# Attention scores from split float32r operands in 32x128 tiles, value products in 128x32 tiles, and another order of the work

## The chip, the cores and the metric

The kernel runs on one core of one Trainium2 chip, in one launch. The metric is the device time in microseconds (us): the median of several executions. The engines of a core work side by side, each through its own queue in order: TensorE (PE; its weight loads PEld are shown apart), VectorE (DVE), ScalarE (ACT), GpSimd (POOL) and SyncE (SP), which here issues nearly all DMA transfers.

## The reference, cut to what matters

A hybrid block on x of 8 sequences x 256 tokens x 512 features, fp32. Four layers follow each other, each adding to x: attention with one set of weights, a feed-forward layer, attention with another set of weights, the same feed-forward layer. Each begins with a layernorm.

```python
xq, xk = rope(q), rope(k)                  # 32 query heads, 8 key/value heads, 16 wide
scores = einsum('bhsd,bhtd->bhst', xq, repeat(xk, 4)) / 4
scores = where(causal, scores, -inf)
probs = softmax(scores)
out = einsum('bhst,bhtd->bhsd', probs, repeat(xv, 4)) @ w_o
...
result = x @ base_w.T + base_b             # feed-forward
result += 2 * lora(x, weights of the two best of 8 experts)
```

## The kernel before, in words

A **unit** is one layer pair (attention and feed-forward) of one sequence: 16 units, in the order of four sequences' first pairs, their second pairs, then the other four sequences. A unit has two token halves t of 128.

Every piece of work is given to a planner by `add(engine, cost, tag, function, reads, writes, take, give)`. At the end `Plan.run` issues all pieces in the order of a hand-kept table of due times, TIMES, one number per piece in the order of the `add` calls; LOANS says which buffer of a pool each piece is lent. The costs in `add` don't act in the run. So the order on each engine is fixed beforehand, across units: scores of one unit stand between projections of another, feed-forward products of a third.

Attention of a unit, with its lines:

- Layernorm of each half; four TensorE transposes (L590) turn it, an ACT copy (L597) writes xnT. One of the 64 layernorms (table TURNED) is turned by DVE and DMA instead.
- k (L618) and v (L629) as products, copied to kvs (L637). k is rotated (DVE L643, L645, POOL L667, L669) and copied by ACT with half of each 32 rows set to zero: kz1 (L674), and kz2 (L678), where a row of ones is put in. v goes to vp with ones beside it, by POOL copies (L660) and DMAs (L663).
- q in two pairs of column blocks (L689), rotated by DVE (L703, L706) and POOL (L709, L711), which writes q(0); a DMA copies it to q(1) (L718).
- **First scores**, for the row maximum: five operations (L744), fp32, in 32x64 tiles (32 rows of the array by 64 columns, eight side by side), queries as weights. ACT copies them from PSUM (L759), POOL masks them (L775), DVE takes the negated maximum nm (L789). nm is transposed (L798), copied (L801) and sent by DMA (L805) into a spare row of each head's q.
- **Second scores**, keys as weights, queries streaming: five operations (L830) in 32x64 tiles over 64-key blocks, the spare row adding the negated maximum. ACT takes the exponential (L845), POOL masks diagonal blocks (L856).
- **Value products** (L875) in 64x32 tiles over 64-key blocks, with the sums of the exponentials in the columns of ones; a diagonal block leaves out the query group that lies before it. ACT copies out (L890); the sums go by DMA (L895) to a DVE reciprocal (L898), by DMA to DRAM (L902) and back spread over partitions into rec (L906). DVE merges the two halves (L909) and multiplies (L913). The output product wo follows (L921), and x is added (L928).

The feed-forward layer has a transposed layernorm, gate and lora products (L942), the gate on DVE, a transpose (L992), the base product (L1006) with the lora product on top (L1012), and the addition to x (L1022).

Tiles: `tile_position=(row, column)` says which part of the 128x128 array a product uses. PSUM has eight banks; a score operation takes two pairs of them, a pair holding two tiles' rows of results.

Of the kernel before, what the change touches and what calls it, by code (L numbers as in the profile page):

```python
# [8 lines left out]
F32 = mybir.dt.float32  # L9
U32 = mybir.dt.uint32  # L10
AF = mybir.ActivationFunctionType
# [13 lines left out]
NBIG = 5  # L25
SPLIT = 16
FIXED = 1.65

TURNED = "0000000000000000000000000000000000000000100000000000000000000000"
# [4 lines left out]
0 620 0 620 4960 1860 2480 3100 4340 5950 6695 7300 7660 3720 9430 10050 12530 29775 43837 42597  # L34
31635 27295 19777 10670 8810 11910 31015 17917 43217 8190 13670 20397 19157 18537 32255 11290 29155
13700 14280 22390 23490 0 2000 3707 4707 5707 8227 1550 5390 6707 14505 3150 4510 4610 4850 5610
5910 7307 8022 3900 5290 5740 5980 6565 6865 7767 8522 12767 14527 15457 16642 17490 17860 26610
21017 17297 21410 20700 21680 22865 22455 23275 23775 9227 10997 16370 15150 17190 19430 16387 19077
21712 21102 24070 25340 30395 26675 28467 30042 31042 32330 33660 36372 31367 34192 33192 35277
37682 40534 38857 38077 40302 39302 41642 42752 48982 44232 41067 43322 42322 44477 45267 46122  # L40
34727 37452 35952 38792 39582 41147 50347 50752 52147 51527 50227 50602 52767 50907 55137 57612
56682 59607 66017 58497 60652 59722 61837 63927 61397 63552 62622 65982 67962 68892 64877 66102
67032 68407 69527 67202 69822 71527 70907 74567 75877 75257 77727 73327 81392 86207 90717 70067
71977 73552 74637 76497 78297 79627 80867 82717 76437 89381 91117 99562 91939 92549 94327 96637
97222 97702 100537 101872 107547 108242 109457 113002 113522 114002 114092 114602 114802 115002
115092 116322 117577 104602 120102 121237 100172 101392 102142 103367 103952 107022 109202 109917
111847 114272 115487 115902 118687 116252 119042 119552 119752 119952 120042 120982 121357 110632
131692 132827 9410 10630 10830 11660 12245 13785 18157 19832 10020 10730 10900 11140 17020 17320
18617 19332 20847 22607 23537 24722 25377 25747 58227 57802 27915 52677 27330 28040 29222 29632
41822 32692 29437 32957 35592 34982 36412 40372 24467 26237 28262 29465 29270 30540 44457 45077  # L50
43967 45192 46192 47477 48807 50204 47327 49482 48552 52947 58497 59672 60284 52237 53462 54962
57117 60727 63639 61962 78097 79322 80252 81547 83047 84352 73297 75502 74572 76587 77957 78812
64757 65132 65437 66057 90837 91372 92297 91677 69047 70752 71682 72767 74917 94617 95842 96772
97857 99947 115352 117757 116577 109662 111817 110887 103582 105162 106092 108817 110727 102102
104232 105317 105937 107737 108187 109427 111277 113352 115302 116602 120357 122072 123982 125557
127262 126642 129217 129667 130287 132137 134177 135737 140192 143947 121847 122457 123167 126562
127239 127577 129172 129887 150102 139232 140487 140822 141597 142462 141952 142752 142552 142952
145167 146592 147187 133542 148482 151437 144557 145692 149347 151372 152047 152347 158672 162477
160762 164732 166847 172472 173707 175252 174642 176012 175812 176212 176302 179172 179811 170322
180262 181557 8800 17320 17420 18460 19540 20332 28007 28722 15760 17150 17250 22970 23555 25222  # L60
32337 35122 36317 39047 40137 41322 43356 43726 73887 41977 53387 71917 46057 46767 64552 59252
61582 54462 48297 50467 53194 53844 54577 55847 42037 44937 48332 49594 50137 51407 58422 57182
79067 81182 82112 84287 85617 87172 82337 84492 83562 86947 88327 91327 92649 85237 87392 86462
90857 91967 94397 95009 101097 102372 103302 106757 109937 110792 89867 91522 92522 95057 95847
97352 100417 100792 108807 101097 115232 115667 116592 115972 125302 126577 128297 137647 140747
137182 140667 142207 143362 145452 132572 133797 134797 129632 132447 130857 143692 146257 144917
147862 148982 149362 151017 152172 152792 154947 157652 155792 159502 153972 164667 165852 172822
150762 152512 154087 157032 155172 165972 166422 167042 168892 158882 173432 175512 179427 174032
175152 176512 176752 178791 179091 181302 182377 180612 183032 184247 186252 189187 186602 189542
190052 190252 190452 190542 193222 194477 183992 199262 200557 180037 180647 180747 181882 184444  # L70
186077 187932 188687 203907 189362 190737 191072 191847 191422 193722 194432 194232 194632 194722
196242 196777 219252 224482 225929 18830 19440 27080 28750 29335 31972 35697 36952 22362 26980 28912
31810 36242 38382 46867 47582 74317 77167 76237 78352 81022 82177 106487 80247 79007 88057 89437
93077 94262 93852 100172 99672 53207 56107 58902 58292 70647 80277 59467 62367 64552 65202 67137
79007 101717 102337 97517 98742 100942 102037 103887 105282 121102 122327 123257 124342 125452
126627 127369 153832 155107 156107 157262 158892 163002 160827 169352 170577 172707 173862 174902
176582 163762 165917 164987 167042 167832 170262 174422 176087 177012 176392 182732 186797 187722
187102 179292 181447 180517 183637 184757 192252 194657 193477 195742 197832 195272 197957 196957
198292 199517 200517 201702 203977 202977 205177 206297 200302 201957 203042 203662 205462 206532
205912 208382 207132 212032 214622 219509 205622 207532 211127 212902 212282 214932 215382 216002  # L80
217852 215212 224716 226332 231336 220119 224616 226539 227422 228286 228857 230112 230827 236052
231662 234347 234682 236052 235332 236859 237369 243667 245012 245102 254592 254967 232782 257162
258427 233694 235162 235262 235502 236117 240507 248562 249277 242902 249992 251367 251767 252287
253237 252727 255412 254632 259647 259737 261052 261557 251112 262382 263677 122557 129047 129147
129387 134047 135797 138152 139987 133437 135537 135637 135877 137002 137302 138772 139487 154852
159292 156772 160477 162632 169447 193582 170132 177632 199922 170432 171142 172297 175177 175587
192047 144662 146712 152177 148737 152997 163462 160222 161992 164017 165362 168622 171852 178252
188342 181762 184427 182987 185877 187207 191512 208852 210127 212127 213212 217722 218897 220729
225362 227517 226587 228732 229842 236247 232016 222892 225547 224117 226632 227942 229026 213652
214877 215807 216892 220252 222407 237972 238347 239892 238652 237692 238497 239272 240512 242762  # L90
244987 243987 246072 253862 245662 247817 246887 249682 251772 249022 252487 253487 254712 255937
256867 258172 260327 259397 261412 262687 255682 257797 258882 259502 261487 262557 261937 264407
260682 269972 271052 274967 259142 263882 265537 267242 266622 269042 270112 269492 271962 269322
275577 282262 286177 276982 277592 277692 281262 282197 282497 288662 289537 287592 291052 292267
292602 294157 293562 294512 302197 300427 302517 302707 305022 305397 301542 306572 307867 286787
287397 287497 288862 290157 291037 292012 292727 295422 296942 298317 300627 301147 303497 302987
306647 306136 306847 306937 307612 308837 298062 324852 325987 310852 326767 153222 155227 155327
158372 169317 171577 173962 174677 182167 182777 182877 183117 183702 185357 187472 188187 209872
212722 211792 213907 214562 216512 249412 235502 233022 232706 218832 219542 221437 228447 233847
221847 190482 193502 195527 196177 202637 214562 196522 202722 205872 206522 209757 221042 222377  # L100
234262 230692 231917 232847 234002 237322 238882 239862 242227 241227 247192 248302 251154 249477
316012 317237 318237 319392 320502 321677 322289 343932 346087 345157 347172 347962 350312 346822
348047 348977 350062 350902 353332 323692 324877 325182 329787 367232 367667 367972 369212 349812
# [991 lines left out]
```

## Time and profile before

| | us |
|---|---|
| median of 3 runs | 775.36 |
| runs | 774.77 to 775.43 |
| span of the profiled execution | 775.9 |
| PE busy, L744 / L830 / L875 | 89.6 / 89.9 / 78.5 |
| PE busy, L689 / L921 / L1006 | 124.5 / 117.0 / 116.4 |

The page gives no time for the profiled execution beyond its span, which lies 0.5 us above the median of the runs. A busy time counts an engine's instructions from start to end, overlaps once; instructions of TensorE overlap, so a line's share is only roughly its cost. "x16" counts instructions: an fp32 product of TensorE is two. The granted TensorE clock has a mean of 0.996. In a timeline a row is a run of like instructions: start, length, engine, line, operation, tile names, tile shape, count, and in brackets the idle time ahead of it and what ended it.

### The profile page before, as it was taken

How to read it: one execution, taken by the hardware profiler on the slowest of the kernel's cores; microseconds unless marked ns; L12 is line 12 of the kernel's file. 1: busy time of each engine (PE TensorE's matmuls, PEld its weight loads, DVE VectorE, ACT ScalarE, POOL GpSimd, SP SyncE). 2: the span in 40 equal slices, each digit the busy share in tenths (PEclk: the TensorE clock that was granted, in tenths of full speed). 3: DMA queues.
4: the chain of work that ended last, by engine and by line, in shares of the span. 5: the costliest groups of instructions: out<-in, count | busy, mean ns of one | idle time of the engine just before them, and what ended most of it. 6: DMA issues, size and time to landing. Idle time of an engine off the chain costs nothing.

```text
span 775.9 us, 18093 instructions
## 1 busy us (share of the span) xinstructions
PE 761.0 (98%) x7192; PEld 410.1 (53%) x7192; DVE 489.4 (63%) x1036; ACT 493.1 (64%) x826; POOL 507.0 (65%) x495
## 2 busy tenths in 40 slices
PE   7999999999999999999999999999999989999998
PEld 6865554564555455546555465355555435444344
DVE  5394866468668547556748468556974883465654
ACT  3679675657767664685665657747478676657631
POOL 3899983677666776466847468664758975646530
PEclk8999999999999999999999999999999999999999
DMA  9631100011010010121022210011001100111111
GB/s 293 174 101 34 35 31 18 17 46 34 17 44 22 3 48 15 37 56 49 30 73 69 68 53 18 5 45 34 16 22 46 56 3 19 39 41 45 31 45 54
DMA packets 49395, 36.59 MB, mean 47 GB/s; under 512 B 30624, under 2 KB 34208, under 8 KB 49312
## 3 DMA queue, kind: packets, MB, share of 16 engines
q1 hardware_dynamic: 48768, 35.42, 15.6%
q8 instruction: 56, 0.92, 0.5%
q14 instruction: 27, 0.22, 0.1%
q10 hardware_dynamic: 544, 0.03, 0.0%
HBM read 19.97 MB, written 4.98 MB: 32 GB/s over the span
## 4 chain that ended last, share of the span: by engine, by line
PE 86%; POOL 5%; issue 3%; ACT 2%; DMA 2%; DVE 1%; SPq 0%; POOLq 0%; ACTq 0%; DVEq 0%
PE banks L689 14%; PE banks L921 13%; PE banks L1006 13%; PE banks L830 9%; PE banks L744 9%; PE banks L875 9%; PE banks L942 4%; PE banks L618 4%; PE banks L590 4%; PE banks L629 3%; PE banks L1012 3%; POOL big L775 2%; POOL big L856 2%; ACT big L845 1%; DMA big<-in_wqkv_a 1%
## 5 line engine op out<-in xcount | busy, mean ns | idle before, releaser
L775 POOL TENSOR_SCALAR_AFFINE_SELECT big<-big 64x1024 f32<-64x1024 f32 (+1 forms) x160 | 170.2, 1063 | 90.8 <-ACT big L759 85.2
L789 DVE TENSOR_REDUCE nm<-big 128x8 f32<-128x512 f32 (+3 forms) x112 | 185.1, 1669 | 47.2 <-POOL big L775 47.2
L759 ACT COPY big<-banks 128x512 f32<-128x512 f32 (+1 forms) x235 | 160.3, 749 | 54.2 <-PE banks L744 50.3
L845 ACT ACTIVATE big<-banks 128x512 f32<-128x512 f32 (+1 forms) x215 | 161.3, 811 | 48.5 <-PE banks L830 44.5
L856 POOL TENSOR_SCALAR_AFFINE_SELECT big<-big 64x1024 f32<-64x1024 f32 (+1 forms) x96 | 142.7, 1488 | 62.3 <-ACT big L845 57.2
L689 PE MATMUL banks<-xnT,wqkv 128*128 128x256 f32 x512 | 124.5, 390 | 0.3 <-ACT big L759 0.3
L921 PE MATMUL banks<-wo,e 128*128 128x512 f32 x256 | 117.0, 600 | 1.0 <-DVE ro L703 0.7
L1006 PE MATMUL banks<-base_sb,yT 128*128 128x512 f32 x256 | 116.4, 598 | 0.0
L689 PEld LDWEIGHTS banks<-xnT,wqkv 128*128 128x128 f32 x512 | 95.0, 193 | 31.7 <-issue 14.7
L830 PE MATMUL banks<-q,kz 32*64 32x512 f32 (+1 forms) x1536 | 89.9, 537 | 2.6 <-ACT lwT L996 1.0
L744 PE MATMUL banks<-kz,q 32*64 32x384 f32 (+3 forms) x2048 | 89.6, 443 | 1.3 <-ACT big L759 1.3
L560 POOL TENSOR_TENSOR st<-st,neg_half 128x1 f32<-128x1 f32 x64 | 35.4, 554 | 75.3 <-DVE st L558 62.4
L875 PE MATMUL banks<-big,vp 64*32 64x512 f32 (+1 forms) x1536 | 78.5, 522 | 0.3 <-ACT big L845 0.3
L563 ACT ACTIVATE xn<-x,st 128x512 f32<-128x512 f32 x64 | 51.9, 817 | 40.0 <-DVE st L561 37.2
L921 PEld LDWEIGHTS banks<-wo,e 128*128 128x128 f32 x256 | 46.4, 190 | 55.9 <-issue 47.7
L1006 PEld LDWEIGHTS banks<-base_sb,yT 128*128 128x128 f32 x256 | 46.3, 190 | 54.0 <-issue 50.1
L744 PEld LDWEIGHTS banks<-kz,q 32*64 32x64 f32 x2048 | 36.6, 130 | 41.0 <-issue 17.0
L875 PEld LDWEIGHTS banks<-big,vp 64*32 64x32 f32 x1536 | 26.2, 106 | 53.9 <-issue 38.6
L554 DVE BATCH_NORM_STATS2 st<-x 128x6 f32<-128x512 f32 x64 | 43.8, 688 | 12.7 <-DMA x<-in_x 11.8
L709 POOL TENSOR_TENSOR ro<-ro,rtab 128x512 f32<-128x512 f32 x32 | 41.2, 1289 | 15.3 <-DVE ro L703 8.4
L890 ACT COPY e<-banks 128x1024 f32<-128x1024 f32 (+1 forms) x39 | 33.1, 864 | 23.1 <-PE banks L875 13.7
L830 PEld LDWEIGHTS banks<-q,kz 32*64 32x64 f32 x1536 | 25.4, 130 | 37.8 <-issue 17.8
(74 smaller groups left out, 876.0 us busy)
## 6 DMA issues: line engine op xcount, KB each, us to landing
q<-q SPq DMA_DIRECT2D x32, 256.0 KB
rec<-recd SPq DMA_DIRECT2D x32, 256.0 KB
x<-in_x SPq DMA_DIRECT2D x16, 256.0 KB
out<-x SPq DMA_DIRECT2D x16, 256.0 KB
big<-in_wqkv_a SPq DMA_DIRECT2D x2, 512.0 KB
big<-in_wq_b SPq DMA_DIRECT2D x2, 512.0 KB
base_sb<-in_base_t SPq DMA_DIRECT2D x4, 256.0 KB
wo<-in_wo_b SPq DMA_DIRECT2D x4, 256.0 KB
```

The source lines that it names most:

```text
L563: add("ACT", 0.82, (u, z + "ln"), lambda: nc.scalar.activation(at("xn", k), xt(b, t), AF.Identity, bias=st(10, 11), scale=st(9, 10)), [xk, ...
L689: nc.tensor.matmul(at("bank", k)[:, (j % 2) * S : (j % 2 + 1) * S], W[:, c, j * P : (j + 1) * P], xnT()[:, c, :], start=(c == 0), stop=(c ...
L744: nc.tensor.matmul(ps[64 * c : 64 * c + 64, base // 256 * 256 : base // 256 * 256 + 2 * dist] .rearrange("p (s k) -> p s k", s=2)[:, :, ba ...
L759: add("ACT", 1.03, (u, f"s1{gr}"), lambda h=h, kb=kb: [nc.scalar.copy(at("big", kb)[:, 2 * h + lo : 2 * h + hi, :], ps) for lo, hi, ps in ...
L775: nc.gpsimd.affine_select(out=v, in_=v, compare_op=ALU.is_ge, fill=MASKED, base=0, pattern=[[0, 2048 // w], [0, blocks * w // 2048], [-1, ...
L789: nc.vector.tensor_reduce(nmv(t)[:, :, m0 : m0 + k, :, g], v, AX.X, ALU.max, negate=True)
L830: nc.tensor.matmul(ps[64 * s : 64 * s + 64, 256 * col : 256 * (col + ng)], kz2()[lo : lo + 32, s, k * P + 64 * h : k * P + 64 * h + 64], q ...
L845: add("ACT", 1.03, (u, f"s2{gr}"), lambda z=z, kb=kb: [nc.scalar.activation(pv_(kb)[:, 2 * z + lo : 2 * z + hi], ps.rearrange("p z (g n) - ...
L856: nc.gpsimd.affine_select(out=v, in_=v, compare_op=ALU.is_ge, fill=0.0, base=0, pattern=[[0, 16 * nm], [1, 64]], channel_multiplier=-1,)
L875: nc.tensor.matmul(ps[s][32 * i : 32 * i + 32, 256 * g : 256 * (g + ng)].rearrange("p (g n) -> p g n", n=256), vp()[64 * s : 64 * s + 64, ...
L921: nc.tensor.matmul(at("bank", ("wo", km)), e()[:, 1, j * P : (j + 1) * P], WO[:, j, :], start=(j == 0), stop=(j == 3),)
L1006: nc.tensor.matmul(ps, at("yT", k)[:, c, :], base_sb[:, c, :], start=(c == 0), stop=False)
```

## The change: what it does

Operands. `half(z)` reads or writes a tile as float32r. A copy into such a view rounds to the part that float32r keeps (high); the value minus it, rounded again, is low.

- k: two shuffles spread each head's 16 rows over 32 (each twice), for s = 0 and 1; ACT writes the high part kh, POOL the low part kl. kz1 and kz2 go.
- q: the rotated q is written in an order with the token blocks outside; ACT writes its high part, DVE its low part, one DMA puts both into DRAM (qd), two fetch them so that each head half s has high and low in alternate rows, 32 rows a head. The copy q(0) to q(1) goes.
- First scores: `qv(s)` times kh, then kl, summed in PSUM; 32x128 tiles, four side by side.
- nm is split in high and low (two DVE operations), transposed together, and sent by one DMA into rows of a tile nmr.
- Second scores: kh, kl, and a third pass of constant selector rows `sel` with nmr, 32x128 tiles, over 128-key blocks, split by s: six operations. The mask is one POOL instruction of 128 partitions per diagonal operation.
- Value products: 128x32 tiles over 128-key blocks, one operation per (t, k, s): six, with nothing left out. vp is written by two POOL copies; its DMAs go.
- The broadcast of the sums goes into the second half of e after the merging copy, and rec goes; the product is made in place. Pools: kvs 2 to 1, nm 4 to 2.
- TURNED goes: every layernorm is turned by TensorE. TIMES and LOANS are new.

```diff
         for s in range(2):
+            add("DVE", 0.45, (u, "krope"), lambda s=s: nc.vector.stream_shuffle(
+                kw()[:, s, :], krc(), [16 * s + d // 2 for d in range(32)]),
+                [(u, "krc")], [(u, "kw", s)], give=[("kr", u)])
+        add("ACT", 0.6, (u, "khl"), lambda: nc.scalar.copy(half(khl(0)), kw()),
...
+        add("POOL", 1.30, (u, "khl"), lambda: nc.gpsimd.tensor_tensor(
+            half(khl(1)), kw(), khl(0), ALU.subtract),
...
+            add("ACT", 0.6, (u, "qhl"), lambda ro=ro, rc=rc: nc.scalar.copy(half(ro()), rc()),
+                [(k, "rc")], [(k, "ro")])
+            add("DVE", 0.69, (u, "qhl"), lambda ro=ro, rc=rc: nc.vector.tensor_tensor(
+                half(rc()), rc(), ro(), ALU.subtract), [(k, "ro")], [(k, "rc")], kind="port")
+            add("SP", FIXED + 1.0, (u, "qhl"), lambda k=k: nc.sync.dma_start(
+                at("qd", k), at("ro", k).rearrange("p h j n -> p (h j n)")),
...
+                    q(s)[:, 2 * jp : 2 * jp + 2].rearrange("p j n -> p (j n)"),
+                    at("qd", k).rearrange("(i s d) (h n) -> s i (d h) n", i=4, s=2, h=2)[s]),
...
+                    for s in range(2):
+                        for h in range(2):
+                            for i in range(4):
+                                lo = 32 * i
+                                ps = at("pair", (kb, i // 2))[i % 2]
+                                nc.tensor.matmul(
+                                    ps[:, base + s * dist : base + s * dist + nk],
+                                    qv(s)[lo : lo + 32, m, 2 * t + g, :],
+                                    half(khl(h))[lo : lo + 32, s, 0:nk],
+                                    start=(h == 0), stop=(h == 1), tile_position=(lo, 0),
+                                )
...
+                for z in range(3):
                     for i in range(4):
                         lo = 32 * i
                         ps = at("pair", (kb, i // 2))[i % 2]
+                        if z < 2:
+                            w = khl(z)[lo : lo + 32, s, k * P : (k + 1) * P]
+                            v = qv(s)[lo : lo + 32, :, 2 * t : 2 * t + 2, :]
+                        else:
+                            w = sel[lo : lo + 32, s, :]
+                            v = half(at("nmr", (u, t)))[lo : lo + 32].rearrange(
+                                "p (g m n) -> p m g n", g=2, m=2)
+                        nc.tensor.matmul(
+                            ps.rearrange("p (g m n) -> p m g n", g=2, m=2), half(w), v,
+                            start=(z == 0), stop=(z == 2), tile_position=(lo, 0),
+                        )
...
+                        for i in range(4):
+                            nc.tensor.matmul(
+                                ps[32 * i : 32 * i + 32].rearrange(
+                                    "p (j g k) -> p g j k", j=4, g=2),
+                                vp()[:, s, k, i, :],
+                                pv_(kb)[:, i].rearrange("p g (j k) -> p g j k", j=4),
+                                start=(k == 0), stop=(k == t), tile_position=(0, 32 * i),
+                            )
```

## The prediction

> **What bounds the kernel now.** I read four views in turn: busy time by engine, the chain that ended last, TensorE alone in order of time, and all engines around one normalisation chain. The first two on the page:
>
> ```profile
> PE 761.0 (98%) x7192; PEld 410.1 (53%) x7192; DVE 489.4 (63%) x1036; ACT 493.1 (64%) x826; POOL 507.0 (65%) x495
> ...
> PE 86%; POOL 5%; issue 3%; ACT 2%; DMA 2%; DVE 1%; SPq 0%; POOLq 0%; ACTq 0%; DVEq 0%
> ```
>
> TensorE is idle for 775.9 - 761.0 = 14.9 us, and the chain lies on it. A third of its work is scores and value products. A "busy" PE includes overlaps, so I price operations from start to start, TensorE alone, in order of time (start us, length us, line, shape, instructions):
>
> ```profile
> 302.50 1.11 PE L744 MATMUL banks<-kz,q 32*64 32x512 f32 x16
> 303.54 1.19 PE L942 MATMUL banks<-gl_sb,yT 128*128 128x136 f32 x8
> ...
> 316.64 3.24 PE L875 MATMUL banks<-big,vp 64*32 64x512 f32 x64
> 319.81 1.11 PE L830 MATMUL banks<-q,kz 32*64 32x512 f32 x16
> 320.86 1.99 PE L618 MATMUL banks<-xnT,wqkv 128*128 128x256 f32 x8
> 322.78 1.12 PE L744 MATMUL banks<-kz,q 32*64 32x384 f32 x32
> 323.83 0.29 PE L798 MATMUL banks<-ident,nm 128*32 128x128 f32 x1
> 323.95 1.06 PE L629 MATMUL banks<-wqkv,xnT 128*128 128x128 f32 x8
> 324.85 3.60 PE L1006 MATMUL banks<-base_sb,yT 128*128 128x512 f32 x8
> 328.28 0.27 PE L992 MATMUL banks<-ident,gl 128*128 128x128 f32 x1
> 328.39 1.06 PE L629 MATMUL banks<-wqkv,xnT 128*128 128x128 f32 x8
> 329.38 1.11 PE L830 MATMUL banks<-q,kz 32*64 32x512 f32 x16
> ```
>
> Four prices come out. (1) An fp32 product is two instructions. Eight of 512 columns take 328.28 - 324.85 = 3.43 us: 0.429 us each, 0.84 ns a column and instruction, 0.857 us a product. (2) Eight instructions with 128 columns and 128 new weight columns take 324.85 - 323.95 = 0.90 us, 0.1125 each. (3) A score operation (16 instructions, eight tiles side by side, so two rounds of 0.429) takes 303.54 - 302.50 = 1.04: 0.857 + 0.18. The value products of one query half (seven full rounds' worth, 3.00) take 319.81 - 316.64 = 3.17: also + 0.17, though four times longer. So tiles run truly side by side and about 0.18 is paid per **run** of tiled work, not per round. (4) The untiled work ahead of a tiled run ends later: L629 takes 0.99 before a score (329.38 - 328.39) against 0.90. Other lines pay up to 0.20 (L618: 1.92 against 8 x 0.215 = 1.72). I use 0.15.
>
> **The change on TensorE, per unit (16 units).** Before: five score operations for the maximum, five for the exponentials, five full-size equivalents of value products (1.5 + 3.5): 15 x 0.857 = 12.86 us.
>
> After, value products: six of four fp32 products, 128x32 tiles, four side by side: 6 x 0.857 = 5.14. It is +0.86 because a 128-key block can't skip the empty half of a diagonal block.
>
> Exponential scores: six operations of three rounds, 512 columns each, float32r. No row shows a float32r pass. The nearest row is one fp32 instruction, 0.429 a round. A quarter of an fp32 product is 0.857/4 = 0.214: an fp32 product multiplies two parts of each operand in two instructions, and the change hands over operands already reduced to one part each, which leaves one of four partial products. I take the quarter for that count; the row's price, half a product, stays as the upper end, and nothing in the trace goes below the quarter. 18 x 0.214 = 3.86, against 4.29.
>
> Maximum scores: groups 0 to 2 have eight rounds of 64 to 192 columns, each with 128 new weight columns. No row of 128 new weight columns is shorter than price (2), so I take 0.1125 a round: 3 x 8 x 0.1125 = 2.70. Groups 3 and 4 have four rounds of 256 columns: 2 x 4 x 0.107 = 0.86. Sum 3.56 against 4.29. From below, at a quarter price throughout, groups 0 to 2 cost 3 x 1024 columns x 0.42 ns = 1.28.
>
> Together 12.56 against 12.86: -0.30, times 16 = **-4.8 us**. Fewer passes are almost eaten by one more score operation, a third pass for the maximum (the sel rows), and one more value product.
>
> **Runs and switches.** Sorting TensorE's operations by the two tables of due times gives 154 runs of scores and 35 of value products before, 157 and 63 after; changes from untiled to tiled work go from 144 to 169. So 3 x 0.18 + 28 x 0.17 + 25 x 0.15 = **+9.1 us**. The sixth value operation and the split by key half s cause it: their weights and masks arrive at different times, and the order lets other work between. A float32r run may pay less or more than 0.18 (its first weights are 128 columns: a load takes 190 ns on L1006, 131 on L744): nothing to twice, +/-28 us over 157 runs.
>
> One layernorm goes back from the DMA to TensorE: **+0.5** (four transposes).
>
> Rule against row: the Trainium skill, "TensorE: Matmul & The Clock Gate", section "Measured speedup vs the span model", has four row tiles of 512 columns only 3.07 times faster, not four. Price (3) has no such loss per round. By that rule the float32r rounds, some 7.4 us a unit, would be 30% longer: about +35 us, an estimate from that page. Its section "The mechanism" lets a weight load overlap only products of another row group. The rounds of L875 in one run show no exposed load; by the rule each of 18 + 32 rounds a unit would show one, with the page's 107 ns for 128 columns about +85 us, again an estimate.
>
> **The other engines.** DVE: 32 shuffles at 0.44 (L643), 32 subtractions at 0.69 (as L706), 64 tiny ones at about 0.16: +46. ACT: four kz passes (rows L674 and L678, 34.8 in all) leave, 48 copies of 128x512 at 0.59 and 16 x 2 exponentials at 1.03 come: +27. POOL: k's subtraction 16 x 1.28 = +20.5; masks 64 x 2.12 = 136 against 142.7. All three stay below 545 us, 70%: none becomes the bound, and TensorE covers their work wherever it has another unit's products next. Without that cover the delay counts.
>
> What lengthens is the path. q used to be ready for scores after the POOL addition (L711). Now a copy (0.59), a subtraction (0.69) and two transfers through DRAM follow. All engines, near the end, price a hop:
>
> ```profile
> 739.31 1.15 SPq L902 DMA_DIRECT2D recd<-sums  x2
> ...
> 741.76 0.61 SPq L906 DMA_DIRECT2D rec<-recd  x1
> ...
> 745.56 0.69 DVE L913 TENSOR_TENSOR e<-e,rec 128x512 f32<-128x512 f32 x1 [1.85 <-DMA rec<-recd]
> ```
>
> The second small write is issued near 739.9 and its reader at 741.76: 1.9. The 256 KB broadcast takes 745.56 - 741.76 = 3.8. So q gains 1.3 + 2 x (1.9 to 3.8) = 5.1 to 8.9 us, say 7; bytes grow by 32 x (1024 - 256) KB, on engines with a 16% share. k gains two shuffles, a copy and a subtraction less two kz passes: about 2. The maxima gain two tiny DVE operations. The output's broadcast (L906) now waits for the masked copy (L909), and what stands behind it on SP waits too; that copy ran at 742.80 here, 1 us after the issue, so about 1 us per half, under other products except in the last units. Transfers of v and the copy q<-q leave; SP's issues stay at eight a unit on this part.
>
> At the start no other unit covers: the first scores stand at 32.46, after q at 29.21. With 7 more they can't start before 36.2: **+4** (0 if products of the next units fill it, 9 if the second unit is late as well). Later, at 600 to 700 us, where the first wave of units runs out, TensorE is idle for 4.1 us; a path longer by about 10 and single instead of double kvs and half as many nm buffers give **+4** more (0 to 25).
>
> **Sum** against the execution's own span: 775.9 - 4.8 + 9.1 + 0.5 + 4 + 4 = 788.7; the median of the runs lies 0.5 below that span, so **788**.
>
> **Rivals.**
> (A) As summed, 780 to 800: 0.52.
> (B) Faster. Weight loads of four row tiles hide behind the round before, so that rounds under 256 columns cost their columns alone: 2.70 becomes 1.28, times 16 = -23, giving 788 - 23 = 765. For it: in L744 eight loads of 64 columns hide in rounds as short as 128 columns (322.78 to 323.83 holds four rounds and still takes 1.05). Against: price (2). It decides from the point where a round of the first three groups costs about 0.08 instead of 0.1125 (384 rounds x 0.033 = 12.7). 0.18.
> (C) The change doesn't get the quarter: a float32r instruction costs as much as an fp32 one, 0.429 a round. 18 x 0.215 + 8 x 0.107 = 4.7 more a unit, +76: 864. For it: the only one-instruction products here, L590's transposes, cost 0.11 per 128 columns. 0.10.
> (D) The longer path or the runs cost several times what I gave: 800 to 825. For it: POOL waits 142 us for ACT behind scores already. 0.13.
> (E) No measurable difference, parts of A and B cancelling: 0.07.
>
> Leaving out C and the lower half of B and the far end of D, the range is 764 to 820. About 0.2% (1.6 us) is what a measurement here can tell from no change. Faster 0.18 (B), same 0.07 (E), slower 0.75 (A, C, D).
>
> **What would show it.** A: exponential scores about 0.64 + 0.18 from start to start, the maximum's first group near 1.08, its last near 0.61; PE busy still 95% or more. B: the first group near 0.65. C: 1.3 + 0.18. D: PE idle over 35 us with q or nmr named. I am wrong if TensorE's runs cost under 0.1, or if idle time falls.

## The result and the profile after

| | median, us | runs, us | ratio to before [95% interval] |
|---|---|---|---|
| before | 775.39 | 774.77 to 775.55 | |
| after | 916.19 | 912.58 to 919.17 | 1.1826 [1.1786, 1.1865] |

The change makes the kernel 18% slower. The profiled execution took 913.86 us, with a span of 912.1. The direction was forecast; the size, 788 with a range to 820, was not.

The page of after: busy time by engine, the granted TensorE clock and the DMA engines' share in 40 slices, and the chain that ended last:

```profile
PE 815.8 (89%) x6044; PEld 474.6 (52%) x6044; DVE 546.6 (60%) x1196; ACT 515.6 (57%) x740; POOL 523.7 (57%) x481
...
PEclk9878999989988999999999999899999998979999
DMA  9432120201102012101221213020120120200001
...
PE 56%; DMA 20%; DVE 12%; ACT 5%; issue 3%; POOL 2%; SPq 2%; DVEq 0%; ACTq 0%; POOLq 0%
```

TensorE falls from 98% to 89% of the span, its clock dips all through the run, and a fifth of the chain lies on transfers, where it was 2%. No other engine is near its limit.

TensorE can be accounted for in full: span = its busy time at full clock + what half clock added (half of the busy time in stretches with a granted clock of 0.50) + its idle time.

| us | span | busy at full clock | added by half clock | idle |
|---|---|---|---|---|
| before | 775.9 | 758.0 | 3.0 | 14.9 |
| after | 912.1 | 776.5 | 39.3 | 96.4 |
| difference | 136.2 | **18.5** | **36.3** | **81.5** |

TensorE's own work, the subject of most of the prediction, is the smallest part. The waits of after that matter, and then the first of them in before (engine, line, waited for, total us, times, longest):

```profile
DVE e L916 <- DMA e<-recd: 73.1, 22, 10.7
...
PE banks L922 <- DVE e L916: 34.7, 13, 7.2
...
PE banks L751 <- DMA q<-qd: 17.8, 4, 7.6
```

```profile
DVE e L913 <- DMA rec<-recd: 25.4, 13, 7.0
```

The largest is not q, whose path got longer, but the broadcast of the softmax sums (e<-recd): DVE waits for it, and the output product (L922) waits for DVE; in before the waits of that product (L921) add up to 1.1 us, none of them for this. One such stall in the chain of waits of after (start, length, what):

```profile
166.56 3.59 DMA qd<-ro
170.16 0.54 SPq L719
...
171.89 10.21 DMA recd<-sums
182.15 3.64 DMA e<-recd
185.81 0.70 DVE e L916
186.65 5.53 PE banks L922 x8
```

The write recd<-sums carries 8 KB, yet lands 10.2 us after it was issued. Just ahead of it SP had issued four fetches q<-qd of 256 KB. Stretches of after around it (busy time and count of PE, PEld, DVE, ACT, POOL; then clock, DMA share, GB/s):

```profile
168.00:170.00 2.00, 2.00 (x24) 1.59 (x21) 1.60 (x1) 0.66 (x2) 2.00 (x3) 1.00 0.79 315
172.00:173.00 1.00, 1.00 (x13) 0.60 (x14) 0.00 (x0) 0.21 (x2) 0.00 (x0) 1.00 0.27 104
180.00:181.00 1.00, 0.00 (x0) 0.00 (x0) 0.00 (x0) 1.00 (x2) 0.00 (x0) 1.00 0.26 100
184.00:185.00 1.00, 0.00 (x0) 0.00 (x0) 0.00 (x0) 0.00 (x0) 0.41 (x1) 0.50 0.49 182
```

While q is written to qd, the DMA engines' share is 0.79. While it is fetched, the share is about 0.26, and the rate 100 GB/s: 256 KB take 2.6 us, four fetches some 10. The fetch reads qd as `"(i s d) (h n) -> s i (d h) n"`: its outermost dimension is four blocks of 32 rows. The Trainium skill, "DMA: Bandwidth & Descriptors", in its rules for kernel authors, says that an outermost dimension of fewer than 16 confines a transfer to at most that many DMA engines; four of 16 is the share seen. From 179.5 on TensorE has nothing to do, and when it goes on at 186.65 it runs at half clock.

TensorE's prices themselves came out close. Timeline of after (start, length, line, shape, count):

```profile
312.69 0.50 PE L843 MATMUL banks<-q,kh 32*128 32x512 f32 x4
313.03 0.40 PE L843 MATMUL banks<-q,kl 32*128 32x512 f32 x4
313.26 0.40 PE L843 MATMUL banks<-nmr,sel 32*128 32x512 f32 x4
313.58 0.66 PE L592 MATMUL banks<-ident,xn 128*128 128x128 f32 x4
314.17 1.06 PE L882 MATMUL banks<-big,vp 128*32 128x512 f32 x8
315.17 0.30 PE L811 MATMUL banks<-ident,nm 128*64 128x128 f32 x1
315.40 1.06 PE L882 MATMUL banks<-big,vp 128*32 128x512 f32 x8
316.40 0.33 PE L751 MATMUL banks<-kh,q 32*128 32x128 f32 x4
...
317.44 0.33 PE L994 MATMUL banks<-ident,gl 128*128 128x128 f32 x1
```

A float32r round of 512 columns takes 0.23 (313.26 - 313.03), a quarter of an fp32 product and a little; an operation of the second scores 0.89 (313.58 - 312.69), a value operation 1.00, the first maximum group 1.04 (317.44 - 316.40) in eight rounds.

### The profile page after: what moved, and what is told of

Read it like the earlier page. It is cut to its first block, busy times and chain, and to the rows that moved or that the text cites. A ratio compares the mean times of both kernels' runs of the same rounds, so it can differ in the third digit from the quotient of the medians.

```text
span 912.1 us, 15854 instructions
## 1 busy us (share of the span) xinstructions
PE 815.8 (89%) x6044; PEld 474.6 (52%) x6044; DVE 546.6 (60%) x1196; ACT 515.6 (57%) x740; POOL 523.7 (57%) x481
## 4 chain that ended last, share of the span: by engine, by line
PE 56%; DMA 20%; DVE 12%; ACT 5%; issue 3%; POOL 2%; SPq 2%; DVEq 0%; ACTq 0%; POOLq 0%
PE banks L922 10%; PE banks L679 9%; PE banks L882 8%; PE banks L1008 7%; DMA e<-recd 6%; PE banks L843 5%; PE banks L751 5%; DMA recd<-sums 4%; DMA q<-qd 4%; DMA qd<-ro 3%; PE banks L592 3%; PE banks L619 2%; PE banks L1014 2%; DVE nm L795 2%; ACT big L765 2%
## 5 line engine op out<-in xcount | busy, mean ns | idle before, releaser
L856 ACT ACTIVATE big<-banks 128x1024 f32<-128x1024 f32 (+1 forms) x207 | 190.7, 963 | 89.1 <-PE banks L843 84.1
L781 POOL TENSOR_SCALAR_AFFINE_SELECT big<-big 64x1024 f32<-64x1024 f32 (+1 forms) x160 | 169.6, 1061 | 116.1 <-ACT big L765 109.2
L765 ACT COPY big<-banks 128x1024 f32<-128x1024 f32 (+1 forms) x176 | 157.1, 943 | 88.9 <-PE banks L751 87.7
L865 POOL TENSOR_SCALAR_AFFINE_SELECT big<-big 128x2048 f32<-128x2048 f32 x64 | 137.7, 2153 | 80.3 <-ACT big L856 73.1
L922 PE MATMUL banks<-wo,e 128*128 128x512 f32 x256 | 128.3, 648 | 35.0 <-DVE e L916 34.7
L679 PEld LDWEIGHTS banks<-xnT,wqkv 128*128 128x128 f32 x512 | 96.3, 195 | 23.5 <-issue 6.8
L882 PE MATMUL banks<-big,vp 128*32 128x512 f32 x768 | 101.1, 630 | 3.2 <-POOL big L865 2.4
L922 PEld LDWEIGHTS banks<-wo,e 128*128 128x128 f32 x256 | 50.4, 206 | 97.9 <-issue 63.8
L581 POOL TENSOR_TENSOR st<-st,neg_half 128x1 f32<-128x1 f32 x64 | 36.2, 570 | 112.8 <-DVE st L579 98.3
L751 PE MATMUL banks<-kh,q 32*128 32x192 f32 (+3 forms) x1024 | 77.4, 308 | 20.8 <-DMA q<-qd 17.8
L751 PEld LDWEIGHTS banks<-kh,q 32*128 32x128 f32 x1024 | 57.9, 201 | 56.5 <-issue 22.2
L751 PE MATMUL banks<-kl,q 32*128 32x192 f32 (+3 forms) x1024 | 68.7, 291 | 0.0
L843 PE MATMUL banks<-q,kh 32*128 32x512 f32 x384 | 55.8, 500 | 4.5 <-ACT big L856 3.5
L751 PEld LDWEIGHTS banks<-kl,q 32*128 32x128 f32 x1024 | 57.3, 203 | 0.0
L843 PEld LDWEIGHTS banks<-q,kh 32*128 32x128 f32 x384 | 22.1, 185 | 55.8 <-issue 29.3
```

The lines of the kernel that those rows point to most:

```text
L679: nc.tensor.matmul(at("bank", k)[:, (j % 2) * S : (j % 2 + 1) * S], W[:, c, j * P : (j + 1) * P], xnT()[:, c, :], start=(c == 0), stop=(c ...
L751: nc.tensor.matmul(ps[:, base + s * dist : base + s * dist + nk], qv(s)[lo : lo + 32, m, 2 * t + g, :], half(khl(h))[lo : lo + 32, s, 0:nk ...
L765: add("ACT", 1.03, (u, f"s1{gr}"), lambda h=h, kb=kb: [nc.scalar.copy(at("big", kb)[:, 2 * h + lo : 2 * h + hi, :], ps) for lo, hi, ps in ...
L781: nc.gpsimd.affine_select(out=v, in_=v, compare_op=ALU.is_ge, fill=MASKED, base=0, pattern=[[0, 2048 // w], [0, blocks * w // 2048], [-1, ...
L843: nc.tensor.matmul(ps.rearrange("p (g m n) -> p m g n", g=2, m=2), half(w), v, start=(z == 0), stop=(z == 2), tile_position=(lo, 0),)
L856: add("ACT", 1.03, (u, f"s2{gr}"), lambda z=z, kb=kb: [nc.scalar.activation(pv_(kb)[:, 2 * z + lo : 2 * z + hi], ps.rearrange("p z (g n) - ...
```

## The experiments

The theory at the start: fetches on a quarter of the DMA engines delay the sums' round trip behind them. The rival: what costs is the longer path itself (more hops and operations), however fast the fetch. Ratios are to the kernel before, timed on the same chip (774.0 to 775.1 us there).

**1. Each fetch as four transfers of 32 rows** (256 issues for 64).

```diff
-    nc.sync.dma_start(q(s)[:, 2*jp : 2*jp+2]..., at("qd", k).rearrange(...)[s])
+    [nc.sync.dma_start(q(s)[32*i : 32*i+32, 2*jp : 2*jp+2]..., at("qd", k).rearrange(...)[s, i])
+     for i in range(4)]
```

> The changed kernel, but each fetch of q from DRAM (four blocks of 32 rows in one transfer, which moved 100 GB/s at a 0.25 share of the DMA engines, 2.6 us each) is four transfers of one block of 32 rows each. Theory 'narrow fetch': the fetches run on a quarter of the DMA engines and hold up what is queued behind them (one 4 KB write of the sums took 10.2 us behind four of them). Then the fetches spread, the idle time of TensorE falls from 96 us to under 40, and the time is 780 to 815 us. Rival 'long path': the added steps from q and k to the scores and the smaller pools make TensorE wait whatever the fetches' speed; then the time stays over 885 us.

870.44 us, ratio 1.1226 [1.1170, 1.1282]: neither theory's number. (The write of the sums carries 8 KB, not the 4 of the expectation.) The chain of this kernel shows why (the first and the last of sixteen issues in a row, then the small write):

```profile
165.83 0.32 SPq L719
...
172.71 0.42 SPq L719
...
173.17 1.77 DMA recd<-sums
```

The small write now lands in 1.8 us instead of 10.2, as the theory has it; but 16 issues of 0.42 us, one after the other, hold SP for 7.3 us (165.83 to 173.12) ahead of it.

**2 and 3. The same bytes, narrow and wide, in the kernel before.** 64 copies of 256 KB from x to unused DRAM, at the place where q is ready; the two kernels differ in the order of the rows alone.

```diff
+    for s in range(2):   # 2: four blocks of 32 rows
+        nc.sync.dma_start(spare[jp].rearrange("(i z r) n -> z i r n", i=4, z=2)[s],
+                          x[b].rearrange("(i z r) n -> z i r n", i=4, z=2)[s])
...
+        nc.sync.dma_start(spare[jp][P*s : P*s+P, :], x[b, P*s : P*s+P, :])   # 3: one block of 128
```

> The kernel before with two more 256 KB copies per q pair (64 in all) from x to an unused DRAM scratch, as four blocks of 32 rows in one transfer; nothing reads the copies and no step of the path changes. 'Narrow fetch' expects that they hold the queue for about 64 x 2.6 = 168 us and delay the sums, the maxima and the copies of q behind them: 800 to 900 us, with waits for the broadcast of the sums. 'Long path' expects 775 to 781, since no path got longer.

> The same as the run with narrow copies, with the same bytes in the same places of the order, but each copy as 128 rows in one block. Both theories expect 775 to 785 us; if it is as slow as the narrow copies, the bytes or the number of transfers matter and not how they spread over the DMA engines.

Narrow: 831.88 us, 1.0734 [1.0696, 1.0771]. Wide: 779.27 us, 1.0063 [1.0045, 1.0080]. Nobody reads these copies, so the 53 us between them come from their shape alone. The waits of the narrow kernel and then of the wide one for the same broadcast, and SP's own for the small write ahead of it:

```profile
DVE e L919 <- DMA rec<-recd: 48.5, 15, 7.9
SPq L912 <- DMA recd<-sums: 48.9, 29, 8.3
```

```profile
DVE e L919 <- DMA rec<-recd: 26.9, 12, 7.3
SPq L912 <- DMA recd<-sums: 28.3, 28, 1.9
```

**4. A wide fetch in the changed kernel.** The columns of q's weights are put in another order, so that the rows that one fetch needs lie together.

```diff
-    at("qd", k).rearrange("(i s d) (h n) -> s i (d h) n", i=4, s=2, h=2)[s]
+    at("qd", k).rearrange("(s r) (h n) -> s (r h) n", s=2, h=2)[s]
```

> The changed kernel with the columns of the q weights ordered by key half s first (16 small copies at the start instead of 8), so that q's rows lie in DRAM as each fetch needs them: one fetch of 128 rows in one block, no further issue, the same bytes. With 32-row fetches SP spent 16 x 0.46 us in a row on issuing, and a write of the sums waited behind that too. Theory 'held queue' (fetches, first by few DMA engines, then by their number, hold the sums and maxima behind them on SP): both hold-ups go, 785 to 815 us, TensorE idle below 40 us. Rival 'long path': the rest of the 96 us over the kernel before belongs to the added steps and smaller pools: over 845 us.

848.42 us, 1.0953 [1.0932, 1.0973]. Its waits for the sums are half of those of after:

```profile
DVE e L917 <- DMA e<-recd: 36.7, 19, 4.5
PE banks L923 <- DVE e L917: 6.2, 6, 1.8
```

The shape of the fetch is worth 68 of the 141 us. That is half: on the number the rival's side was met, and the theory holds for the other half only.

**5. Small issues in the kernel before.** 192 transfers of 2 KB, as many as experiment 1 had over the change (`for s in range(6): nc.sync.dma_start(spare[s], x[b, 0:16, 0:32])` behind the same addition).

> The kernel before with six more transfers of 2 KB (DRAM to an unused DRAM scratch) per q pair, 192 in all: the issues that 32-row fetches add to the changed kernel, nearly without bytes and on no path. 'Held queue' expects 192 x 0.46 = 88 us more issuing on SP, in knots of 2.8 us, to show as 785 to 820 us with waits for the sums; 'long path' expects under 780.

801.32 us, 1.0344 [1.0313, 1.0375]. Issues alone cost 27 us. With 1 and 4 it roughly fits: splitting cures the shape like the wide fetch, and pays 870 - 848 = 22 for its 192 issues.

**6 to 9. The wide fetch without transfers.** Each leaves work out of kernel 4: the write and fetch of q in all units but the first on each buffer (6); the sums' round trip with the reciprocal (7); the maxima's transfer (8); all three (9).

```diff
-    ..., lambda ...: nc.sync.dma_start(
+    ..., lambda ...: fetched() and nc.sync.dma_start(      # 6; None in 7 and 8
```

> The kernel with wide fetches (848 us) without the transfers of q to DRAM and back, but for the first unit in each of the three attention buffers; later units score with the q that lies there. All engine work stays. Theory 'q detour': what is left over the prediction's 788 us is the detour's two hops and its hold on SP (SP waited 76 us for the q subtraction and 41 us for the write): 785 to 805. Rival 'sums behind each other on DVE' (the product with the sums waits for its broadcast and holds the gates behind it): within 8 us of 848.

> The kernel with wide fetches without the round trip of the softmax sums (five transfers and the reciprocal); DVE's merge and product stay, with what lies in e. Theory 'sums on DVE' expects 790 to 815, since no product waits 37 us in all for a broadcast; 'q detour' expects 835 or more.

> The kernel with wide fetches without the transfer of the maxima into nmr, which stays zero; the maxima are still worked out, turned and copied. 'Q detour' and 'sums on DVE' both expect 838 to 848; if it falls below 825, the maxima's path, which starts after the first scores, is what the longer q path pushes out.

> All three left out at once: q's detour, the sums' round trip and the maxima's transfer. If transfers and the queue are the whole rest, TensorE's own work is left: 775.9 - 14.9 + 4.8 + about 10 for longer runs = 776, plus start and end: 778 to 795. If it stays over 815, the rest lies in the engines' own order and waits and not in transfers.

| kernel | median, us | ratio [95% interval] | against kernel 4 |
|---|---|---|---|
| 6 | 843.61 | 1.0911 [1.0875, 1.0946] | -5 |
| 7 | 837.40 | 1.0814 [1.0792, 1.0835] | -11 |
| 8 | 847.74 | 1.0941 [1.0909, 1.0972] | -1 |
| 9 | 837.16 | 1.0815 [1.0791, 1.0840] | -11 |

Kernel 4's own runs spread from 847.1 to 853.2, so the rows of 6 and 8 show little or nothing. Once the fetch is wide, leaving out these transfers gains 11 us, and 63 us over the kernel before remain without them.

**10 and 11. Without the splitting as well.** From kernel 9, 10 also leaves out what DVE does for the low parts (q's subtraction, the split of the maxima); 11 also DVE's shuffles and the ACT and POOL instructions for high and low of q and k, in all units but the first on each buffer.

> The kernel without the three round trips (837 us), less what the change adds on DVE for the low parts: the 32 subtractions of q and the 64 small operations on the maxima. The scores then use stale or zero operands. In its profile TensorE waited about 7 us for the maxima's split and 10 us for the gates on DVE. Theory 'busy DVE': those waits and the half clock after them go, 805 to 822 us. Rival 'order of the work': the new due times leave such gaps whatever DVE does, 830 or more.

> As the run before, and also without the copies to high parts on ACT, the shuffles of k on DVE and the subtraction on POOL, but for the first unit in each attention buffer. 'Busy DVE' expects no more than 10 us under the run before; a theory 'added steps on the path' expects 785 to 800, near TensorE's own work (about 775 at full clock); 'order of the work' expects 820 or more.

10: 827.22 us, 1.0684 [1.0645, 1.0723]. 11: 827.10 us, 1.0690 [1.0645, 1.0734]. DVE's part is worth 10 us, the rest nothing. What TensorE still waits for in kernel 9 and then in kernel 11:

```profile
PE banks L998 <- DVE gl L993: 8.9, 6, 2.5
PE banks L815 <- DVE nm L813: 7.5, 5, 2.5
```

```profile
PE banks L998 <- DVE gl L993: 8.9, 6, 2.5
PE banks L755 <- ACT big L769: 4.5, 10, 0.7
PE banks L847 <- ACT big L860: 2.7, 5, 0.7
```

The split of the maxima (nm) goes, as it must; the gate (gl) and short waits for ACT's copies and exponentials stay, work that the kernel before has too.

**12. A busier DVE in the kernel before:** two reductions of 128x512 more after each rotation of q, 64 in all and 44 us, that nobody reads (`nc.vector.tensor_reduce(spare, wqkv_sb[0][:, 0, 0:D], AX.X, ALU.add)`).

> The kernel before with 64 more DVE reductions of 128x512 behind the two q operations, 64 x 0.68 = 44 us of DVE work that nothing reads: about what the change adds there. 'Busy DVE' expects 785 to 800; 'order of the work' expects 774 to 780, because the old order has the slack.

786.50 us, 1.0141 [1.0112, 1.0170]: 12 us, though DVE is at 68% only. So work on an engine far from its limit is not free here. That it delays what stands behind it in DVE's order is the likely way; no run singles it out.

**13 and 15. Whose queue?** In the changed kernel, with its narrow fetches, ScalarE issues the small transfers (13: L906 and L913) or the fetches (15: L719) in place of SP: `nc.sync` becomes `nc.scalar`.

> The changed kernel with one edit: the write of the reciprocals to DRAM (recd<-sums) and the broadcast back (e<-recd), 96 small issues in all, are given by ScalarE instead of SyncE; the narrow q fetches stay on SyncE. Theory 'order in SyncE's queue': the small transfers no longer stand behind the fetches, the sums write falls from up to 10.2 us to about 2, the waits of DVE for e<-recd fall from 73 us to under 40, and the time falls from 916 to between 840 and 885 (no further than the wide fetch's 848, and with about 96 x 0.5 = 48 us more issuing on ScalarE, of which some shows). Rival 'the DMA engines themselves are occupied by the narrow fetches, whichever queue a transfer comes from': the write stays near 10 us and the time stays above 900.

> The changed kernel with one edit: the 64 narrow fetches q<-qd are given by ScalarE instead of SyncE; their shape stays as it is, four blocks of 32 rows. Theory 'order in SyncE's queue': SyncE is free for the sums, and the time falls from 916 to between 840 and 890, though ScalarE then waits for the qd write ahead of each fetch and DVE or TensorE waits for ScalarE instead. Rival 'occupied DMA engines': above 900.

13: 904.96 us, 1.1663 [1.1639, 1.1688]. 15: 915.29 us, 1.1831 [1.1798, 1.1864]. The theory that the place in SP's queue decides isn't borne out by the times: parting the small transfers from the fetches gains 11 us in one kernel and nothing in the other. The chain of kernel 13, then its stretches:

```profile
172.70 3.72 DMA recd<-sums
...
179.16 7.05 DMA e<-recd
...
187.46 5.36 PE banks L922 x8
```

```profile
178.00:180.00 2.00, 2.00 (x17) 1.03 (x10) 0.57 (x2) 0.16 (x1) 1.84 (x2) 1.00 0.26 102
180.00:182.00 2.00, 1.89 (x17) 1.04 (x15) 0.00 (x0) 1.82 (x3) 0.71 (x1) 1.00 0.44 159
182.00:184.00 2.00, 0.00 (x0) 0.00 (x0) 0.00 (x0) 1.88 (x2) 0.05 (x1) 1.00 0.28 97
184.00:186.00 2.00, 0.00 (x0) 0.00 (x0) 0.00 (x0) 0.00 (x0) 2.00 (x1) 0.51 0.23 76
```

The small write is quicker (3.7 for 10.2), so the queue does count for it; but the broadcast, now free of SP, takes 7.05 instead of 3.64. It ends at 186.2, where it ended at 185.8 in after. The broadcast is narrow itself: its view, `to_broadcast([8, 16, D])`, has eight blocks outermost, and where it ran alone in after its share was 0.49 (184 to 185). Here the share rises to 0.44 after its issue and falls back to 0.28, that of the fetches, until it ends. That fits a transfer part of which goes through at once while the rest waits on the engines that the fetches occupy; the trace doesn't show single engines. The Trainium skill, "DMA: Bandwidth & Descriptors", states that issuing engines share the same 16 DMA engines (section "Issuing engines are not separate DMA queues"); these two runs agree, with 11 us and nothing gained.

The two runs do not price the queue alone, since each moves waits elsewhere. Of kernel 13, then of kernel 15:

```profile
PE banks L922 <- DVE e L916: 17.3, 7, 5.6
ACT big L856 <- DMA recd<-sums: 15.5, 4, 7.3
```

```profile
PE banks L922 <- DVE e L916: 21.3, 8, 8.2
PE banks L751 <- DMA q<-qd: 27.7, 6, 9.2
```

TensorE waits less for the sums' product in both (34.7 in after), but in 13 ScalarE's exponentials stand behind the small writes, and in 15 TensorE waits longer for q (17.8 in after). The write recd<-sums is narrow too: its view has four blocks outermost, in the kernel before as well. What a wider write and broadcast would gain, no run tried.

**14. The same for the wide fetch:** L907 and L914 of kernel 4 issued by ScalarE.

> The kernel with the wide fetch (848 us), with the reciprocals' write and the broadcast back given by ScalarE instead of SyncE. Theory 'what the sums' round trip still costs there (11 us, by the run without it) is standing in SyncE's queue': 837 to 844. Rival 'it is the round trip's own length': 846 to 860, since ScalarE has 96 more issues of about 0.5 us.

852.63 us, 1.1020 [1.0987, 1.1053]: no gain. On the number the rival is met, and what the sums still cost there would be the round trip's own length; ScalarE's exponentials waiting 7.1 us for the small writes are part of the time, so this isn't shown apart.

**16. The wide fetch in another order:** kernel 4 with new TIMES and LOANS, which group scores and value products and give later due times to what waits on transfers.

> The kernel with the wide fetch (848 us), all operations the same, issued in another order with other due times and buffers: scores and value products grouped so that there are fewer changes between tiled and untiled work, and later due times for what waits on transfers. Theory 'the gaps and the half clock after them come of the order': at least 12 us less than 848, 815 to 836, idle time of TensorE under 40 us. Rival 'they come of the operations themselves (thin TensorE work, longer chains, fewer buffers), whatever the order': 840 to 865.

862.38 us, 1.1130 [1.1107, 1.1153]: worse by 14, with idle time 51.5 for 47.5. The rival's number was met; but one poor order doesn't show that there is no better one.

What TensorE's accounts say of the main steps:

| us over before | span | own work | half clock | idle |
|---|---|---|---|---|
| after | 136.2 | 18.5 | 36.3 | 81.5 |
| 4, wide fetch | 75.5 | 17.7 | 25.2 | 32.6 |
| 9, and no transfers | 58.7 | 15.6 | 19.6 | 23.5 |
| 11, and no splitting | 47.9 | 16.0 | 13.3 | 18.6 |

Each row is one profiled execution. That of kernel 4 is the longest of its runs, 4.7 us above their median, and that of kernel 11 the shortest, so the steps between rows are good to about 5 us.

## Why the prediction was wrong, point by point

- **What bounds the kernel.** Right for before. It didn't stay so: "TensorE covers their work" is the sentence that failed.
- **Columns and rounds (-4.8), runs and switches (+9.1).** The quarter price held: 0.23 a round against 0.214; the first maximum group 1.04 against 1.08; a value operation 1.00 against 0.857 + 0.14 to 0.17. The second scores took 0.89 against 0.64 + 0.18: 0.05 more in rounds and 0.02 in the run, 96 times, 7 us. TensorE's own work rose by 18.5 where these two terms and the extra layernorm gave 4.8; the other 7 I couldn't assign to lines. Rivals B and C are refuted by these rows.
- **The rules weighed.** A 30% longer round would be 0.28; it is 0.23. An exposed load in each round of the second scores would show as 0.32 by the page's figure, and as 0.40 by the 185 ns that a load of L843 takes in after; the round from 313.03 to 313.26 shows neither. The maximum's rounds do take 0.11 where 128 columns at the quarter price are 0.054: as price (2) had it. Rounds of 192 columns take the same 0.11 (rows of L751 at 324.92, 325.03 and 325.14), so it isn't the columns that set their pace; that the new weights do is the likely reading.
- **Other engines.** DVE +57 (46 forecast), ACT +23 (27), POOL +17 (14). "None becomes the bound" is right, and it isn't enough: without DVE's part 10 us go (experiment 10), and 44 us of DVE in the kernel before cost 12 (experiment 12).
- **The start (+4).** First scores at 35.35 (36.2 forecast); idle time in the first 45 us 10.0 against 4.0, so +6. The size is near, but by luck: the idle time comes after the first scores, in waits of 3.81 and 2.27 us for the next fetches of q (L751 at 39.82 and 42.54), and with the wide fetch (experiment 4) it is 5.4, so +1.3. Most of the +6 is the fetch's shape, which this term did not hold.
- **"Two hops at 1.9 to 3.8", bytes "on engines with a 16% share".** This step failed. The hops were priced by their latency and by a mean share over the span. The fetch's access pattern was in the diff, and its outermost four was not read: each fetch runs at a share of 0.25, four in a row take 10 us, and what shares the DMA engines with them is late, as the 10.2 us of the small write show. This is the part that the runs show: 68 us. I counted only q's own delay, where the dearest one is that of the sums.
- **Later idle time (+4, 0 to 25).** This is the term that was mis-sized: after the first 45 us TensorE's idle time rose by 75.5 (10.9 to 86.4). Rival D had the sign to look for ("PE idle over 35 us with q or nmr named"), but 800 to 825 was too low, and q with 17.8 us of waits is the lesser part.
- **Half clock** had no term. It is 36 us; in the stall shown it sets in some 4 us after TensorE ran out of work at 179.5.

What is settled: the narrow fetch is worth 68 us (experiment 4), and a narrow shape costs by itself, with the queue and the bytes unchanged (2 against 3); issuing from another engine gives back 11 us or nothing (13, 15); the transfers left out beyond that are worth 11, DVE's splitting 10. What stays open: the last 52 us (median of 11 against before), of which TensorE's accounts name 16 as own work, 13 as half clock and 19 as idle time in gaps of up to 2.5 us. Whether a better order, or kvs and nm with the old number of buffers (not tried), would close these gaps, the runs don't tell. No version beat the kernel before.

## What to carry to other kernels

Read a new transfer's outermost dimension before its bytes, and look at the DMA share of its own stretch, not the mean: a transfer on a quarter of the engines delayed small ones that have nothing to do with it, and a broadcast issued from another engine too. Where an engine is full to 98%, a change that thins its work and lengthens the paths around it must be priced by the gaps, not by its passes: here the gaps and the half clock after them cost six times what the passes did. More, smaller transfers are no free cure, since each issue takes its place on the issuing engine.

## What the runs showed of the hardware that was not expected

- Half clock without a long pause. The granted clock changes in steps of 3.41 us and was 0.50 for 97 us in all in after, against 6.8 before. In kernel 4 short gaps are enough:

```profile
468.00:470.00 2.00, 1.42 (x39) 1.11 (x33) 0.00 (x0) 2.00 (x3) 1.94 (x2) 1.00 0.54 187
470.00:472.00 2.00, 1.81 (x13) 0.83 (x10) 1.71 (x1) 2.00 (x3) 1.94 (x3) 0.74 0.62 159
472.00:474.00 2.00, 2.00 (x4) 0.88 (x3) 1.43 (x3) 2.00 (x4) 1.86 (x3) 0.50 0.94 348
```

  TensorE is idle for 0.58 and 0.19 us, among rounds of the first scores, and the clock halves. A gap of 0.98 us among full products in before, at 637.6, did not bring it on. How much idle time or thin work it takes, these runs don't settle.
- A fetch with four outermost blocks: share 0.25, 100 GB/s, against 0.79 and 315 GB/s for the write of the same bytes.
- An issue of the fetches takes SP 0.42 to 0.54 us, one after the other: 192 issues that nobody waits for cost 27 us.
- Float32r in 32x128 tiles, four side by side: 0.23 us a round of 512 columns, 0.11 a round with 128 new weight columns and 128 or 192 columns.
